# A query pipeline seven slots deep instead of nine, with a written timetable for its fill

## The chip, the core and the metric

The kernel runs on one core of one Trainium2 chip. The metric is the device time of one execution in microseconds (us). Three executions of the kernel before took 2966.6, 2970.59 and 2973.62 us; their median, 2970.59 us, is the time before.

The engines are called as the profile calls them: PE multiplies matrices (PEld loads its weights), DVE is the vector engine, ACT the scalar engine with the function tables, POOL the general one, SP the queue from which this kernel issues all its DMAs.

## The reference, cut to what matters

The input x has 8 sequences of 1024 tokens with 512 channels. It is normalized once, and two branches read the result: an encoder layer with Performer attention (16 heads of 32 channels, 128 random features) and an MLP of width 2048, and a channel mix that looks one token back.

```python
xn = _layernorm(x)                                     # no gain, no shift
# attention: phi(u) = exp(u @ omega.T - |u|^2/2 - max) / sqrt(128) + 1e-6
pq, pk = phi(q * 32**-0.25), phi(k * 32**-0.25)        # per head, per token
kv, z  = pk.T @ v, pk.sum(tokens)                      # over the whole sequence
h      = ((pq @ kv) / (pq @ z)) @ wo
a = layernorm(xn + h) * ln1_g + ln1_b
a = layernorm(a + gelu(a @ w1 + b1) @ w2 + b2) * ln2_g + ln2_b
# channel mix: p is xn one token back, zero at the start
r, k = sigmoid((mu_r*xn + (1-mu_r)*p) @ W_r), (mu_k*xn + (1-mu_k)*p) @ W_k
out = x + a + r * (square(relu(k)) @ W_v)
```

## The kernel before, in words

**Arithmetic.** Every large product is made from 16-bit halves: a value is held as a high and a low fp16 part, and a product is three matmuls (high x high, high x low, low x high). `mm3` (L139) is the unit of PE work: 12 matmuls of 128x512 over four chunks of 128 channels. Most engine work before and after it makes such pairs: ACT writes the high half, DVE or POOL subtracts to get the low one.

**Phase one, keys and channel mix.** Tokens come in tiles of 128 (`NU` = 64) and blocks of 512. Pools open and close around two phases that do not fit in memory together. In phase one each slot of 15.4 timetable microseconds (`us`, L191) normalizes a tile, makes V, a K projection (`proj_a`, tile name psu with weights whk), its features in two halves (`KB`, tile pj), and adds them into kv (`KC`, tile kac). Every eighth tile ends a sequence: `KD` and `KE` normalize kv and z of a head group and store them to DRAM (zd, epd). The channel mix, 192 `mm3` units named psk, psr and psf (`ffn_k`, `ffn_r`, `ffn_o`), is spread over the slots by the list `spots` (L904); its inputs come from `mix` (L550), and its results go to DRAM (ffd).

**Phase two, queries and MLP.** Query work is done per item i, which is a group of four heads over one block of 512 tokens; there are 64. An item goes through:
- `Lq`: load the block's normalized transposed tokens (tile xq, 1 MB, one buffer; every fourth item). The tile lies where phase one's pools lay.
- `proj_a`: one `mm3` (psu, weights whq); ACT and DVE make the pair u; SP writes it to DRAM (ud) and issues a DMA transpose of it.
- `proj_l`: three DMAs read ud back in another layout (skq). `norm`: POOL, ACT and DVE turn the transposed u into the squared norms (nsqq).
- `QB`, four times (t = 0 to 3): four small matmuls (pj<-oms,skq), DVE takes the maximum and the bias, ACT the exponentials, and a DMA transpose delivers the features (pq). pj has two buffers, eq three, pq four.
- `QD`, twice: 24 small matmuls with kv (acn<-zq,pq), then DVE divides. `QE`: ACT, POOL and a DMA transpose give oT.

For every block, four `O` units (pso, one per 128 tokens) apply wo; DVE adds the residual (x1), `bstat` and `rstat` make the layer norm, `pre` applies it and transposes the result into x1b. The MLP takes 64 slots, four per block n: in each, four `mlp1` units (psw0) with a GELU on ACT, and four `mlp2` units (acc, four PSUM banks). `fin_a` to `fin_b` finish and store a block.

**What sets the order.** Every step is an event with a time, `at(tau, ...)`; events are issued in order of tau. PE's instructions are chained in that order (`chained`, L129). DVE, ACT, POOL and SP are chained too (`Pinned`, L178), except between `unpin` at TK = 72.55 and `tail_banks` at TM = 81.6: there a list scheduler of the compiler orders them. Each engine then executes strictly in its order, waiting on semaphores. In the MLP slots `warp(j, t)` (L207) maps a place t in the nominal slot j (27.68 long, table `slot_pe`) to a tau, skipping PE work that the slot does not have.

Before, item i has its projection in MLP slot i-9, its features in slot i-8 and its products with kv in slot i-7. `O` of a block takes two slots, two units each.

Of the kernel before, what the change touches and what calls it, by code (L numbers as in the profile page):

```python
# [10 lines left out]
F32 = mybir.dt.float32  # L11
# [28 lines left out]
NU = NB * 8  # L40
# [11 lines left out]
TC = 78.8  # L52
TM = 81.6
QT = (0.68, 0.77, 0.86, 0.95)
QDT = (0.27, 0.49)
QDF = (0.45, 0.75)
QF = (0.10, 0.30, 0.52, 0.90)
# [3 lines left out]
def block_kernel(ctx, tc, x, wq, wk, wv, wo, om3, ln1_g, ln1_b, w1, b1, w2, b2,  # L61
# [84 lines left out]
    def tail_banks():  # L146
        for key in ("act", "dve", "gps", "spq"):
            pin[key] = None
# [46 lines left out]

    def slot_pe(j):
        q = j + 8
        o = 2 if j % 4 in (1, 2) and 0 < j < 59 else 0
        f = j < 4 * NBK
        return [(0.0, MM3 * f), (2.56, MM3 * f), (5.12, MM3 * (j > 0)), (7.68, 0.6 * (q - 1 < NU)),  # L200
                (8.28, MM3 * (q + 1 < NU)), (10.84, MM3 * f), (13.4, 0.6 * (q - 1 < NU)), (14.0, MM3 * o),
                (16.56, MM3 * f), (19.12, 0.22 * (q < NU)), (19.34, MM3 * (j > 0)), (21.9, 0.22 * (q < NU)),
                (22.12, MM3 * f), (24.68, 0.22 * (q < NU)), (24.9, MM3 * f), (27.46, 0.22 * (q < NU))]
# [18 lines left out]
    def Y(j, t):  # L222
        return 0 if j is None else (warp(j, t),)
# [180 lines left out]
    def proj_a(kind, b, u, j=None):  # L404
# [10 lines left out]
        yield us(2.65) if kind == "k" else Y(j, 10.9)  # L415
        u2 = st([128, 2, BLK], F16, "u2", U2_BUFS)
        act.activation(u2[:, 0, :], ps, AF.Copy, scale=sc)
        yield us(1.2) if kind == "k" else Y(j, 11.6)
        dve.scalar_tensor_tensor(u2[:, 1, :], ps, sc, u2[:, 0, :], ALU.mult, ALU.subtract)
        yield us(1.2) if kind == "k" else Y(j, 12.5)  # L420
# [6 lines left out]

    def norm(kind, b, u, j=None):
# [4 lines left out]
        yield us(4.0) if kind == "k" else Y(j, 27.68 + 7.2)  # L433
        act.activation(uu, uu, AF.Square, scale=1.0 / SU)
        yield us(5.0) if kind == "k" else Y(j, 27.68 + 9.6)
# [114 lines left out]
    def mix(bk, p, f):  # L550
# [5 lines left out]
        for w in range(2):  # L556
# [3 lines left out]
            yield us(2.0)  # L560
            df = st([128, BLK], F32, "df", 1)
            gps.tensor_tensor(df, xs[:, 1:BLK + 1], xs[:, 0:BLK], ALU.subtract)
            yield us(4.5)
            for nm, mu in (("k", muk), ("r", mur)):
                dve.scalar_tensor_tensor(
                    xm[nm][:, w], df, mu[:, c:c + 1], xs[:, 0:BLK], ALU.mult, ALU.add
                )
                yield us(2.0 * f)
            yield us(2.0 * f)
        cs = slice(p * 2, p * 2 + 2)  # L570
        for nm in "kr":
# [4 lines left out]
            yield us(3.0)  # L576
            dve.tensor_tensor(m[:, 1, cs, :], xm[nm], m[:, 0, cs, :], ALU.subtract)
            yield us(2.0 * f)
# [41 lines left out]
    def QB(b, u, t, j=None):  # L620
# [3 lines left out]
        sk, nsq = stk["q", b, u], nrm["q", b, u]  # L624
# [4 lines left out]
        yield Y(j, p + 0.3)  # L629
        mx = st([128, 4], F32, "mxq", 4)  # L630
        dve.tensor_reduce(mx, pj, AX.X, ALU.max)
        yield Y(j, p + 1.05)
        bi = st([128, 4], F32, "biq", 4)
        dve.scalar_tensor_tensor(bi, mx, -1.0 / (SU * SU), nsq[:, t * 4:t * 4 + 4], ALU.mult, ALU.add)
        yield Y(j, p + 1.3)
# [4 lines left out]
        yield Y(j, p + (3.9 if t == 0 else 3.1))  # L640
        eng = dve if QLO[t] == "v" else gps
        eng.tensor_tensor(eq[:, 1], e, eq[:, 0], ALU.subtract)
        yield Y(j, p + (5.3 if t == 0 else 4.2))
# [440 lines left out]
```

## Time and profile before

| | |
|---|---|
| median of three runs | 2970.59 us |
| profiled execution: time, span | 2970.69 us, 2968.9 us |
| PE busy | 2787.5 us (94%), 18784 matmuls |
| DVE, ACT, POOL busy | 2264.2, 1767.8, 1026.3 us |
| DMA | 839348 packets, 494.82 MB, mean 167 GB/s |
| end of the last matmul before the span's end | about 28 us |

The profile is one execution, taken by the hardware. Its page has busy time by engine, the span in 40 slices of 74 us each, the costliest groups of instructions and what the engine waited for before them. Because helpers issue all instructions, all matmuls stand under L137 and nearly all other instructions under L185; so they are told apart by tile names. "out<-in" names the tiles written and read, without buffer numbers. A bracket after a row is the idle time before it and what ended it. Landing is the time from a DMA's issue to its completion. Since PE's matmuls overlap, a busy PE is not a PE at full speed: the granted clock (1.0 is full) stands beside it.

### The profile page before, as it was taken

The page shows a single profiled execution, that of the slowest core. Times are in us where ns is not written, and L with a number is a line of the kernel's source. Part 1 is how long each engine was busy: PE and PEld are TensorE (multiplying, and loading weights), DVE is VectorE, ACT ScalarE, POOL GpSimd, SP SyncE. Part 2 cuts the span into 40 slices and gives each one's busy share as a digit, 9 for nine tenths or more (in the row PEclk, how much of TensorE's full clock was granted, in tenths as well). Part 3 has the DMA queues.
Part 4 walks back from the last instruction along what each step waited for, and adds up shares of the span by engine and source line. Part 5 has one row for each costly group of instructions (what it writes and reads, how often), then busy time and mean ns, then how long its engine had stood idle before and what let it go on. Part 6 is the DMA issues. An engine that isn't in the chain of part 4 may idle for free. (4 is left out here: it accounts for less than half of the span.)

```text
span 2968.9 us, 52134 instructions
## 1 busy us (share of the span) xinstructions
PE 2787.5 (94%) x18784; PEld 1390.3 (47%) x18784; DVE 2264.2 (76%) x4308; ACT 1767.8 (60%) x3892; POOL 1026.3 (35%) x945
## 2 busy tenths in 40 slices
PE   3999999999999785999999999999999999999996
PEld 1454445445555342444444444444444444444442
DVE  5888888888888656667777777778777777787554
ACT  4888888888888564455455455454554554554210
POOL 3454555555655233223223223223223232232111
PEclk7999999999999896999999999999999999999998
DMA  6566666666665288877777777777777687786432
GB/s 195 144 171 183 175 176 176 183 179 178 171 172 128 95 184 176 196 162 175 190 164 179 179 169 176 187 163 176 186 171 172 173 175 172 174 179 156 117 100 85
DMA packets 839348, 494.82 MB, mean 167 GB/s; under 512 B 632016, under 2 KB 718128, under 8 KB 837040
## 3 DMA queue, kind: packets, MB, share of 16 engines
q1 hardware_dynamic: 839088, 491.49, 66.6%
q8 instruction: 147, 2.41, 0.4%
q14 instruction: 113, 0.93, 0.1%
HBM read 226.95 MB, written 113.38 MB: 115 GB/s over the span
## 5 line engine op out<-in xcount | busy, mean ns | idle before, releaser
L137 PE MATMUL psw<-x1b,w1s 128*128 128x512 f16 x3072 | 696.5, 380 | 1.8 <-DVE u L185 1.8
L137 PE MATMUL acc<-w2h,gg 128*128 128x512 f16 x2048 | 648.1, 379 | 0.0
L137 PEld LDWEIGHTS <-w1s 128*128 128x128 f16 x3072 | 296.5, 98 | 346.3 <-issue 6.0
L137 PEld LDWEIGHTS <-gg 128*128 128x128 f16 x3072 | 292.7, 98 | 324.1
L185 ACT ACTIVATE g<-psw,b1t 128x512 f32<-128x512 f32 x256 | 173.0, 686 | 374.8 <-PE psw L137 363.5
L137 PE MATMUL acc<-w2l,gg 128*128 128x512 f16 x1024 | 387.9, 379 | 0.0
L185 ACT ACTIVATE e<-pj,biq 128x128 f32<-128x128 f32 x1024 | 291.0, 369 | 149.3 <-DVE biq L185 120.3
L185 ACT ACTIVATE e<-pj,bik 128x128 f32<-128x128 f32 x1024 | 287.9, 391 | 47.7 <-DVE bik L185 47.6
L185 POOL TENSOR_TENSOR eq<-e,eq 128x512 f16<-128x512 f32 x128 | 164.7, 1287 | 385.5 <-ACT eq L185 229.3
L185 DVE TENSOR_REDUCE mxq<-pj 128x4 f32<-128x512 f32 x256 | 175.5, 687 | 119.8 <-PE pj L137 118.7
L185 POOL TENSOR_TENSOR u<-ot,u 128x512 f16<-128x512 f32 x64 | 84.4, 1319 | 460.7 <-ACT u L185 422.1
L185 POOL TENSOR_TENSOR e<-u 128x512 f32<-128x512 f16 x128 | 163.9, 1281 | 107.2 <-DMA u<-u 92.0
L185 ACT ACTIVATE u<-psu 128x512 f16<-128x512 f32 x128 | 75.9, 593 | 207.8 <-PE psu L137 207.7
L185 DVE SCALAR_TENSOR_TENSOR gg<-g,gg 128x512 f16<-128x512 f32 x256 | 189.1, 739 | 8.8
L185 DVE TENSOR_SCALAR gg<-g 128x512 f16<-128x512 f32 x256 | 108.0, 422 | 104.6 <-ACT g L185 104.5
L137 PE MATMUL psv<-whv,xb 128*128 128x512 f16 x512 | 165.9, 386 | 18.7 <-ACT u L185 18.7
L137 PE MATMUL psu<-xb,whk 128*128 128x512 f16 x512 | 156.1, 387 | 28.7 <-DVE v L185 23.3
L185 POOL TENSOR_TENSOR xf<-xf,be 128x512 f32<-128x512 f32 x64 | 81.0, 1265 | 291.8 <-DMA xf<-in_x 172.5
L185 DVE SCALAR_TENSOR_TENSOR ekl<-e,ekh 128x1024 f16<-128x1024 f32 x128 | 177.3, 1385 | 4.5 <-ACT ekh L185 4.4
L185 ACT ACT_TABLE_LOAD x114 | 146.3, 1283 | 55.8 <-DVE biq L185 47.7
L137 PE MATMUL psr<-whfr,mx 128*128 128x512 f16 x512 | 165.9, 386 | 6.6 <-DVE v L185 3.9
L185 POOL TENSOR_TENSOR x<-x,bb 128x512 f32<-128x512 f32 x64 | 89.3, 1397 | 226.1 <-ACT u L185 165.6
(164 smaller groups left out, 5801.9 us busy)
## 6 DMA issues: line engine op xcount, KB each, us to landing
w1s<-w1d SPq DMA_DIRECT2D x256, 256.0 KB, 3.0
ud<-u SPq DMA_DIRECT2D x128, 256.0 KB, 2.2
skk<-ud SPq DMA_DIRECT2D x192, 128.0 KB, 2.8
skq<-ud SPq DMA_DIRECT2D x192, 128.0 KB, 3.2
xt<-in_x SPq DMA_DIRECT2D x64, 256.0 KB, 3.4
xnd<-xt SPq DMA_DIRECT2D x64, 256.0 KB, 2.4
xtd<-xb SPq DMA_DIRECT2D x16, 1024.0 KB, 5.2
ffd<-rsg SPq DMA_DIRECT2D x64, 256.0 KB, 2.2
```

The costliest lines, as they stand in the source:

```text
L137: return chained("pe", nc.tensor.matmul(*a, **k))
L185: return lambda *a, **k: chained(self.key, f(*a, **k))
```

## The change

All matmuls, vector instructions and DMAs of the computation stay; the change is in the order, in a few buffer counts, and in two more loads of the activation table.

- **Depth.** Item i's projection now stands in MLP slot i-7 (`LAG`), after the first psw0, and its features at the end of the same slot. Its products with kv stand in slot i-6, the first of them 2.56 later in the slot. Seven items, not nine, are projected before the first MLP unit.
- **Output projections.** The four `O` units of a block stand in one slot (j % 4 == 2), and `bstat`, `rstat`, `pre`, the final norms and their DMAs get new places.
- **Fill.** `unpin` is gone: all engines stay chained. Projections of items 0 to 6 stand at TQ + 0, 5.1, 10.2, 18.3, 29.1, 39.9, 50.7 (`PSQ`), an item's features start at 15.2 + 10 i, one QB per 2.5; `O` of block 0 stands at 74 to 82, the MLP starts at 102 instead of 9 slots of 15.4 (138.6).
- **Channel mix.** `spots` end with a list `wide` in the fill; `mix` is timed by shares of its interval. Between the last K projection and the first query projection there are 13 units instead of 15, from then to the first psw0 18 instead of 13, before both 161 instead of 164.
- **Smaller.** `KE` of the last sequence stands 2.6 later; xn has 3 buffers instead of 2, x1 10 instead of 11; new clock `rt`, which counts real PE time in a slot.

```diff
-TC = 78.8
-TM = 81.6
+TC = TQ + 73.0 / 15.4
+TM = TQ + 102.0 / 15.4
...
     def tail_banks():
-        for key in ("act", "dve", "gps", "spq"):
-            pin[key] = None
...
+    LAG = 7
+
     def slot_pe(j):
-        q = j + 8
-        o = 2 if j % 4 in (1, 2) and 0 < j < 59 else 0
+        q = j + LAG < NU
+        d = j + LAG - 1 < NU
+        o = 4 if j % 4 == 2 and j < 4 * NBK - 4 else 0
         f = j < 4 * NBK
-        return [(0.0, MM3 * f), (2.56, MM3 * f), (5.12, MM3 * (j > 0)), (7.68, 0.6 * (q - 1 < NU)),
-                (8.28, MM3 * (q + 1 < NU)), (10.84, MM3 * f), (13.4, 0.6 * (q - 1 < NU)), (14.0, MM3 * o),
-                (16.56, MM3 * f), (19.12, 0.22 * (q < NU)), (19.34, MM3 * (j > 0)), (21.9, 0.22 * (q < NU)),
-                (22.12, MM3 * f), (24.68, 0.22 * (q < NU)), (24.9, MM3 * f), (27.46, 0.22 * (q < NU))]
+        return [(0.0, MM3 * f), (2.56, MM3 * q), (5.12, MM3 * (j > 0)), (7.68, MM3 * f), (10.24, 0.6 * d),
+                (10.84, MM3 * f), (13.4, 0.6 * d), (14.0, MM3 * o), (16.56, MM3 * f), (19.12, 0.22 * q),
+                (19.34, MM3 * (j > 0)), (21.9, 0.22 * q), (22.12, MM3 * f), (24.68, 0.22 * q),
+                (24.9, MM3 * f), (27.46, 0.22 * q)]
...
+    def rt(j, t):
+        warp(j, 0.0)
+        ln = warps[j][1]
+        return TM + j + t / ln if t < ln else rt(j + 1, t - ln)
+
+    def Y(j, t, dt):
+        return us(dt) if j is None else (warp(j, t),)
+
+    def R(j, t, dt):
+        return us(dt) if j is None else (rt(j, t),)
...
-        yield us(2.65) if kind == "k" else Y(j, 10.9)
+        yield us(2.65) if kind == "k" else R(j, 5.2, 2.65)
-        yield us(1.2) if kind == "k" else Y(j, 11.6)
+        yield us(1.2) if kind == "k" else R(j, 6.0, 0.8)
-        yield us(1.2) if kind == "k" else Y(j, 12.5)
+        yield us(1.2) if kind == "k" else R(j, 6.8, 0.8)
...
+    def sqt(j):
+        if j is None or j % 4 > 1:
+            return R(j, 18.2 if j and j % 4 == 2 else 13.95, 0.8)
+        return Y(j, 19.0, 0)
...
-        yield us(4.0) if kind == "k" else Y(j, 27.68 + 7.2)
+        yield us(4.0) if kind == "k" else R(j, 11.8 if not j else (14.4, 14.4, 14.4, 13.0)[j % 4], 1.5)
-        yield us(5.0) if kind == "k" else Y(j, 27.68 + 9.6)
+        yield us(5.0) if kind == "k" else sqt(j)
...
-    def mix(bk, p, f):
+    def mix(bk, p, m0, m1):
+        def to(share):
+            return (m0 + share * (m1 - m0),)
...
-            for nm, mu in (("k", muk), ("r", mur)):
+            for nm, mu, f in (("k", muk, 0.21), ("r", mur, 0.28)):
+                yield to(f + 0.36 * w)
                 dve.scalar_tensor_tensor(
                     xm[nm][:, w], df, mu[:, c:c + 1], xs[:, 0:BLK], ALU.mult, ALU.add
                 )
-                yield us(2.0 * f)
-            yield us(2.0 * f)
+            yield to(0.36 + 0.36 * w)
...
-        sk, nsq = stk["q", b, u], nrm["q", b, u]
+        sk = stk["q", b, u]
...
+        nsq = nrm["q", b, u]
+        assert len(nsq.shape) == 2, (b, u, t, j)
...
-        yield Y(j, (8.4, 14.05)[p])
+        yield Y(j, 10.9, 0.7) if p == 0 else R(j, 14.05, 0.7)
...
-        yield Y(j, 16.5)
+        yield R(j, 15.95, 0.7)
...
-        xns[i] = sm_([128, D], F32, "xn", 2)
+        xns[i] = sm_([128, D], F32, "xn", 3)
...
-        x1 = sm_([128, D], F32, "x1", 11)
+        yield us(2.7) if tev is None else (tev,)
+        x1 = sm_([128, D], F32, "x1", 10)
...
-        yield Y(j, (2.7, 5.3, 13.5, 19.2)[k])
+        yield Y(j, 19.2, 0) if k == 3 else R(j, (2.7, 10.3, 13.5)[k], 0)
-        yield Y(j, (4.2, 6.0, 15.2, 23.2)[k])
+        yield Y(j, 23.2, 0) if k == 3 else R(j, (4.2, 12.0, 15.2)[k], 0)
...
-    def unpin():
-        for key in ("act", "dve", "gps", "spq"):
-            pin.pop(key, None)
...
-            at(i + 9 + us(7.65 if b < NB - 1 else 0.0), KE, b, u - 4)
+            at(i + 9 + us(7.65 if b < NB - 1 else 2.6), KE, b, u - 4)
...
-    spots = [c + us(o) for c in range(CM0, CM0 + 72) for o in (0.0, 5.12, 12.0)]
-    spots = [t for k, t in enumerate(spots) if k % 9 != 8]
+    PSQ = (0.0, 5.1, 10.2, 18.3, 29.1, 39.9, 50.7)
+    wide = [2.4 + 2.7 * k for k in range(24)]
+    wide = [TQ + us(t) for t in wide if min(abs(t - q) for q in PSQ) > 1.4]
+    spots = [c + us(o) for c in range(CM0, 73) for o in (0.0, 5.12, 12.0)]
+    spots = [t for t in spots if t < TQ - 0.05]
+    n = 12 * NBK - len(wide)
+    spots = [spots[k * len(spots) // n] for k in range(n)] + wide
...
-                at(m1, mix, bk, 1, ((tau - 0.3 - m1) * 15.4 - 19.0) / 14.0)
+                m1 = max((m0 + tau - 0.3) / 2, tau - 2.4)
+                at(m0, mix, bk, 0, m0, m1)
+                at(m1, mix, bk, 1, m1, tau - 0.3)
...
-    at(TK, unpin)
...
-        s, j = TQ + i, i - 9
+        j = i - LAG
         if j < 0:
-            e = 0.45 if i else 0
+            q = TQ + us(PSQ[i])
+            z = TQ + us(15.2 + 10.0 * i)
             if u % NG == 0:
-                at(s + 0.30 - e, Lq, b, u)
-            at(s + 0.31 - e, proj_a, "q", b, u)
-            at(s + 0.32 - e, proj_l, "q", b, u)
-            at(s + 0.96 - e, norm, "q", b, u)
+                at(q - us(0.1 if i == 0 else 8.0), Lq, b, u)
+            at(q, proj_a, "q", b, u)
+            at(q + us(6.6), proj_l, "q", b, u)
+            at(q + us(8.5), norm, "q", b, u)
         else:
             if u % NG == 0:
-                at(warp(j - 1, 11.0) if j else s - 0.4, Lq, b, u)
-            at(warp(j, 8.28), proj_a, "q", b, u, j)
-            at(warp(j, 15.6), proj_l, "q", b, u)
-            at(warp(j, 18.0), norm, "q", b, u, j)
+                at(rt(j - 1, 5.4) if j else TQ + us(70.0), Lq, b, u)
+            at(warp(j, 2.56), proj_a, "q", b, u, j)
+            at(rt(j, 9.6), proj_l, "q", b, u)
+            at(rt(j, 11.6 if j else 9.4), norm, "q", b, u, j)
         if u == 0:
-            at(s + 1.05, Lz, b)
+            at(z if i == 0 else rt(j, 8.0), Lz, b)
         for t in range(4):
+            if j < 0:
+                at(z + us(2.5 * t), QB, b, u, t)
+            else:
+                at(warp(j, (19.12, 21.9, 24.68, 27.46)[t]), QB, b, u, t, j)
+        for p in range(2):
             if j + 1 < 0:
-                at(s + 1 + QF[t], QB, b, u, t)
+                at(z + us((12.6, 18.6)[p]), QD, b, u, p)
             else:
-                at(warp(j + 1, (19.12, 21.9, 24.68, 27.46)[t]), QB, b, u, t, j + 1)
-        for p in range(2):
-            if j + 2 < 0:
-                at(s + 2 + QDF[p], QD, b, u, p)
-            else:
-                at(warp(j + 2, (7.68, 13.4)[p]), QD, b, u, p, j + 2)
-        if j + 2 < 0:
-            at(s + 2.80, QE, b, u)
+                at(warp(j + 1, (10.24, 13.4)[p]), QD, b, u, p, j + 1)
+        if j + 1 < 0:
+            at(z + us(20.0), QE, b, u)
         else:
-            at(warp(j + 2, 15.4), QE, b, u, j + 2)
+            at(rt(j + 1, 15.3), QE, b, u, j + 1)
...
-                tau = TQ + 6.5 + 0.3 * (t // 2) + 0.01 * (t % 2)
-                at(tau - 0.001, Ln2, t)
+                tau = TQ + us(74.0 + 2.6 * t)
+                at(TQ + us(73.2 + 0.2 * t if t < 3 else 77.0), Ln2, t)
                 at(tau, O, n, t)
-                at(TQ + 7.2 + 0.02 * t, bstat, "P", n, t)
+                at(tau + us(2.75), bstat, "P", n, t)
                 if t % 2:
-                    at(TQ + 7.21 + 0.02 * t, rstat, "P", n, t - 1)
-                at(TQ + 7.3 + 0.15 * t, pre, n, t)
+                    at(tau + us(3.6), rstat, "P", n, t - 1)
+                at(TQ + us((81.2, 81.9, 86.5, 87.2)[t]), pre, n, t)
             else:
-                j = 4 * n - 3 + t // 2
+                at(rt(j - 2, 6.0 + 0.3 * t if t < 3 else 17.0), Ln2, n * 4 + t)
+                at(warp(j - 2, 14.0 + 0.64 * t), O, n, t, warp(j - 2, 14.66 + 0.64 * t))
+                at(max(rt(j - 2, (17.35, 20.0, 23.1, 25.1)[t]), warp(j - 2, 14.67 + 0.64 * t)), bstat, "P", n, t)
-            at(warp(j - 3, 17.4), bstat, "P", n, 1)
-            at(warp(j - 2, 7.2), rstat, "P", n, 0)
-            at(warp(j - 1, 3.4), pre, n, 2, [warp(j - 1, t) for t in (7.0, 7.1, 12.7, 13.3)])
-            at(warp(j - 1, 10.4), pre, n, 3, [warp(j - 1, t) for t in (12.1, 12.2, 16.4, 17.6)])
+            at(rt(j - 2, 20.8), rstat, "P", n, 0)
+            at(rt(j - 2, 27.95), rstat, "P", n, 2)
...
+            for t, c in enumerate((
+                ((2, 33.5), (2, 34.2), (2, 35.2), (3, 6.8), (3, 7.6)),
+                ((3, 1.2), (3, 2.0), (3, 4.9), (3, 7.5), (3, 8.3)),
+                ((3, 8.2), (3, 8.9), (3, 9.7), (3, 13.2), (3, 14.0)),
+                ((3, 9.6), (3, 10.3), (3, 11.1), (3, 16.45), (3, 17.3)),
+            )):
+                w = [rt(j - 4 + r, v) for r, v in c]
+                at(w[0], pre, n, t, w[1:])
...
-            tau = warp(s, (0.0, 2.56, 10.84, 16.56)[k])
+            tau = warp(s, (0.0, 7.68, 10.84, 16.56)[k])
-                at(tau - 1.0 if fc > 3 else TM - 5.0 + fc, get_w1, n, fc)
+                at(tau - 1.0 if fc > 3 else TM - us(20.0 - fc), get_w1, n, fc)
...
-                at(warp(j + 5, (1.3, 7.2, 10.5, 12.7)[t]), bstat, "F", n, t)
-            at(warp(j + 5, 20.4), rstat, "F", n, 0)
+                at(rt(j + 5, (1.3, 6.8, 7.65, 8.5)[t]), bstat, "F", n, t)
+            at(rt(j + 5, 9.35), rstat, "F", n, 0)
...
```

## The prediction

> **What bounds the kernel now.** I read the page's slices first: where does PE not run, or run cold?
>
> ```profile
> PE   3999999999999785999999999999999999999996
> ...
> PEclk7999999999999896999999999999999999999998
> ```
>
> PE is full almost everywhere; the holes are the start, slices 14 to 16 (the hand-over from keys to queries) and the end. The stretches that follow are cut at the last K items, at the first query projection and at the first MLP unit.
>
> ```profile
> core 0: us, PE busy (x) PEld busy (x) DVE busy (x) ACT busy (x) POOL busy (x), PEclk, DMA share, GB/s
> ...
> 972.00:1036.00 64.00, 47.44 (x341) 23.53 (x340) 44.22 (x61) 34.74 (x75) 19.14 (x18) 0.87 0.27 82
> 1036.00:1181.00 145.00, 98.82 (x778) 51.63 (x777) 88.94 (x198) 77.10 (x203) 46.97 (x39) 0.81 0.84 187
> ...
> 1205.00:2900.00 1695.00, 1685.08 (x10816) 825.85 (x10815) 1277.32 (x2703) 824.24 (x1688) 434.86 (x339) 1.00 0.71 168
> ```
>
> Busy time flatters PE, so I count work by spacing at full clock: an mm3 unit in the timeline takes 2.59 us from start to start (psf at 1033.42, next unit at 1036.01), the small pj, acn and kac matmuls 0.055, 0.025 and about 0.028 us each. Then the **drain** (972 to 1036) holds 14 units, 32 pj and 141 kac matmuls = 42 us of work in 64: 22 lost. The **fill** (1036 to 1181) holds 26 units, 130 pj, 336 acn = 83 us in 145: 62 lost. In the **main stretch** PE issues without holes; its waits sum to about 10 us, and with small gaps I count 14. What is lost in the drain and fill, and to whom:
>
> ```profile
> PE kac L137 <- DVE kvz L185: 14.8, 4, 9.0
> ...
> PE pj L137 <- ACT e L185: 23.0, 8, 7.2
> PE acn L137 <- DMA pq<-eq: 22.2, 5, 7.1
> ```
>
> The first row is the drain's, the others the fill's. Only the start, these two stretches and the last 28 us offer time; start and end are not touched. The rest is PE work that the change keeps, unit for unit.
>
> **The change part by part.** The sum is made on the profiled execution, 2970.7 us (span 2968.9), equal to the median to 0.1.
>
> *Drain.* Two psr units now stand between the last feature groups, where before PE had nothing:
>
> ```profile
> 982.48 0.61 PE L137 MATMUL pj<-oms,skk 96*128 96x128 f16 x8
> 984.67 0.61 PE L137 MATMUL pj<-oms,skk 96*128 96x128 f16 x8 [1.58 <-ACT e L185]
> 994.24 0.60 PE L137 MATMUL kac<-kvz,ones 128*128 128x132 f16 x2 [8.96 <-DVE kvz L185]
> 994.63 1.06 PE L137 MATMUL psk<-mx,whfk 128*128 128x512 f16 x2
> ```
>
> From zmean (978.98) to the ready kvz (994.24) DVE needs 15.3 us; PE now has 9.6 us of work there instead of 4.4, so of the 9 us some 5 stay, and of the later waits (2.0 and 4.3) perhaps 2. But the three units that stood after the last kac are gone: the projection follows it at once, and its input can only be loaded when the last store of phase one has landed:
>
> ```profile
> 1027.06 0.32 SPq L185 DMA_DIRECT2D epd<-eps  x1
> ...
> 1030.13 0.32 SPq L185 DMA_DIRECT2D xq<-xtd  x1
> ```
>
> xq landed 4.8 us after its issue (1034.94); the last kac ended at 1026.72. So PE will stand 8.2 us, now uncovered. Everything behind it on PE waits with it (units of the channel mix too), and on SP ud and skq queue behind xq. After a hole the clock is low: the psk unit at 994.63 took 5.0 us instead of 2.59, 2.4 us more. Lost after: 5 + 2 + 8.2 + 2.4 = 17.6, against 22. I take -5. Bounds: no wait but the hole (8.2 lost) -14; all old waits and the hole, +6. The trace is nearest to the middle, since the DVE chain is the same work.
>
> The Trainium skill (TensorE: Matmul & The Clock Gate, Part 1) says that an idle window of about 3.4 us halves the clock and that a busy one of that length restores it, so it speaks against the naked hole; by it the price of the hole's cold restart is at most 1.7 us instead of the row's 2.4, and the sum 0.7 lower.
>
> *Fill.* PE's work from first projection to first psw0 becomes 7 + 18 + 4 = 29 units, 112 pj, 288 acn = 88.5 us. The timetable gives it 102. Can the others keep that pace? Durations of the main stretch's rows: ACT 112 exponentials at 0.28, 28 copies at 0.62, the rest, about 76 us; DVE 84; POOL 44; SP 45 transposes at 1.25 and 21 skq at 0.45 plus the rest, about 80. All fit, none with much to spare. DMA does not fit:
>
> ```profile
> skq<-ud SPq DMA_DIRECT2D x27, 128.0 KB, 2.5
> ud<-u SPq DMA_DIRECT2D x9, 256.0 KB, 2.6
> ...
> pq<-eq SPq DMA_TRANSPOSE x30, 3.3
> ...
> u<-u SPq DMA_TRANSPOSE x9, 3.0
> oT<-u SPq DMA_TRANSPOSE x6, 3.3
> x1b<-u SPq DMA_TRANSPOSE x4, 2.8
> ```
>
> Before's fill kept the DMA engines busy for 0.84 x 145 = 122 us with 49 transposes; the new one has 45 (28 + 7 + 6 + 4), so 122 x 45/49 = 112 us, more than 102. At a share of 0.95 it takes 118. Lost: 118 - 88.5 = 29.5 instead of 62: **-32.5**. Ends: the timetable is kept (packets are stretched by crowding, so 112 may be too much), -48; the features come at before's pace of some 3.9 us a QB (32 between 1046 and 1172), 15 + 28 x 3.9 + 28 = 152 us, +2. I take the DMA share, because it counts the same transfers. Five channel-mix units move here from places with no slack: nothing by themselves, being counted in the work.
>
> The Trainium skill (DMA: Bandwidth & Descriptors, Latency and other measured facts) gives 261 GB/s for DMA transposes, which makes one of 256 KB an estimated 1.0 us and all 45 only 45 us; by it DMA would not bind, the timetable would hold and the sum would be lower by 16.
>
> *Main stretch.* Three things change. (1) Features in the slot of their projection. After psu, PE has acc, psw0, acn, psw0, acn, psw0 = 11.6 us before the first pj waits for skq (22 in the slot with pso). The chain: at the first projection before, psu started at 1036.01 and pj ran at 1046.37 without a wait, so at most 7.6 us after psu's 2.76. In the main stretch add up to 1.5 us for ACT's and DVE's queues (a GELU pair is ahead), and behind DVE's u wait SP's ud, the transpose and skq; in slot j % 4 == 3 two x1b transposes (2.5 us) stand between. That is 8 to 11.5 us: covered. Not so every fourth slot, where xq goes out just ahead of ud:
>
> ```profile
> 1245.21 0.32 SPq L185 DMA_DIRECT2D xq<-xtd  x1
> 1247.12 0.32 SPq L185 DMA_DIRECT2D ud<-u  x1
> ```
>
> Here ud landed 5.9 us after its issue; over the 13 such pairs it was 4.1 to 6.8, elsewhere in the middle 2.15. That brings the chain to about 11.5 to 13 us, and all that PE has in order behind pj (acc, the other pj, psw0) waits with it: I price 0.5 us in 14 slots, 7 us, plus 3 for jitter elsewhere. (2) QD's first half comes 2.56 later: it gains most of the 6.8 us that acn waited for pq in the main stretch, say 4. (3) Four pso in a row: DVE must clear one per 2.59 us (0.69 us each, 2.1 us of layer norm between); with two psum banks the slack is 1.8 us, and I put it at nothing. DVE's work in that slot is about 33 of 35 us; if a wait comes, the next pso bears it. The first MLP slots get 1 us less cover, no price; two more table loads (1.28 each) are hidden by ACT's 49% idle time. x1's smaller pool, xn's third buffer, edits of final norms: off PE's path, nothing. Sum 7 + 3 - 4: **+6**. Bounds: all waits go, -10; a microsecond in each of the 43 short slots, +43.
>
> *Phase one.* 164 against 161 units, `mix` moved: DVE and ACT are at 85 to 87% there and PE loses about 43 us in 824. Nothing, -6 to +6.
>
> Sum: 2970.7 - 5 - 32.5 + 6 = **2939**.
>
> **Rivals.**
> - *The timetable holds* (2924): fill at 102. For it: no engine but PE (88.5) is over 84 us. Against: 0.84 of DMA busy already at a slower pace.
> - *The fill is not compressed* (2960 to 2972): the order is fixed but the pace is DMA's and the pq ring's, as in before, where pq waits were 22 us and pj waited 23 on ACT. For it: share 0.84 over the whole fill; against: that time was spent partly behind a bad order, with 39 us between the last pso and the first psw0.
> - *Slower: the same-slot features starve PE* (about 2985 to 3005). Place: the first pj of a slot, waiting for skq. Each microsecond over the 11.6 of cover costs 43 us over the short slots; against a gain of 37.5 it decides from 0.9 us a slot, a chain of 12.5. For it: ud and skq landings are 2.2 and 3.2 at best, SP is a single queue, and DMA is busy at 0.71; against: the measured 7.6.
>
> **How the numbers follow.** Forecast case (2925 to 2957) 0.56; timetable held or better 0.11; fill hardly shorter 0.16 (of it 0.10 faster, 0.05 same, 0.01 slower); starvation 0.17. Faster by over 0.2% (6 us, about what a measurement of this kernel can tell from no change) 0.77, within 0.05, slower 0.18. The range 2912 to 2978 leaves out about 0.06 below (drain, fill and main all at their good ends give 2899) and 0.14 of the starvation case above. The forecast's own range is 2925 to 2957.
>
> **What would show it.** Right: the fill from first whq projection to first psw0 takes 110 to 125 us with DMA share over 0.9; a PE hole of about 8 us ahead of the first whq projection, ended by xq; in the main stretch pj waits for skq in every fourth slot, under 1 us each, and acn waits shrink. Wrong: pj waits of a microsecond in all short slots, or psw0 and pso waiting for DVE's x1, or a fill over 140.

## The result: slower, 3101.0 us

The changed kernel takes 3101.03 us (median of 4 runs, 3099.33 to 3103.01), the kernel before beside it 2971.12: a ratio of 1.0439, 95% interval 1.0421 to 1.0457. The forecast was 2939. The profiled execution took 3100.28 us, its span is 3098.5. In the changed file all matmuls stand under L133 and the other instructions under L179.

First the slices of the page after, PE busy and granted clock:

```profile
PE   4999999999998858999999999999999999999997
...
PEclk8999999999999878999999999999999999999998
```

They look hardly different: the same two dark slices, and nines after them. Work per stage tells more. I count it as in the prediction (full-clock work by the spacing of matmuls, 2737.6 us in both kernels) and call lost what a stage takes beyond it. K phase is from 148 us to 64 us before the first whq projection, the drain is those 64, the fill ends at the first psw0, the main stretch 105 us before the last matmul.

| lost, us | before | after | change | forecast |
|---|---|---|---|---|
| start, to 148 us | 59.0 | 57.6 | -1.4 | 0 |
| K phase | 43.2 | 33.6 | -9.6 | 0 |
| drain | 21.9 | 18.4 | -3.5 | -5 |
| fill | 62.0 | 71.2 | +9.2 | -32.5 |
| main stretch | 16.4 | 159.8 | +143.4 | +6 |
| last 105 us of matmuls | 0.3 | 0.6 | +0.3 | 0 |
| behind the last matmul | 28.4 | 19.6 | -8.8 | 0 |

The changes add up to 129.6 us, the difference of the two spans. So the question is the main stretch. Drain, fill, first 50 us and main stretch of the changed kernel, by stretches of the trace:

```profile
core 0: us, PE busy (x) PEld busy (x) DVE busy (x) ACT busy (x) POOL busy (x), PEclk, DMA share, GB/s
945.00:1009.00 64.00, 48.62 (x363) 24.70 (x362) 48.27 (x68) 40.18 (x89) 25.51 (x25) 0.93 0.24 73
1009.00:1168.50 159.50, 103.82 (x748) 52.29 (x747) 91.84 (x187) 76.74 (x189) 42.86 (x35) 0.81 0.69 154
1168.50:1219.00 50.50, 42.81 (x278) 20.24 (x279) 21.41 (x44) 18.91 (x37) 7.09 (x6) 0.91 0.76 190
1219.00:2969.00 1750.00, 1651.59 (x10461) 800.57 (x10460) 1307.57 (x2643) 807.91 (x1682) 431.89 (x335) 0.97 0.66 159
```

The main stretch ran without holes at a clock of 1.00 before; now PE is 98 us idle in it and the clock is 0.97. The waits of PE there (1200 to 2950), in us, times and longest:

```profile
PE pj L133 <- ACT e L179: 47.9, 14, 4.0
PE pso L133 <- DVE x L179: 44.5, 13, 4.6
PE pj L133 <- DMA skq<-ud: 6.7, 5, 4.5
```

Two waits, each once per block of four slots, each some 3.5 us. The wait that I feared (pj for skq) is small; that for pq, 6.8 before, is gone. To see in which slots they fall, I took the start of the first psw0 unit of each MLP slot from the timeline and averaged slots 4 to 55 by place in the block (13 each). DVE busy is the time in which at least one of its operations runs; neighbouring ones overlap a little, so the sum of their durations is larger (26.1 us in slot 3 after, the figure in the expectation of e2_late_bb2):

| slot j % 4, us | before | after | DVE busy before | DVE busy after |
|---|---|---|---|---|
| 0 | 26.0 | 25.6 | 20.8 | 16.1 |
| 1 | 30.6 (2 pso) | 25.5 | 21.5 | 20.9 |
| 2 | 30.6 (2 pso) | 40.9 (4 pso) | 25.1 | 31.0 |
| 3 | 25.4 | 31.1 | 20.3 | 24.7 |
| block | 112.6 | 123.1 | 87.7 | 92.7 |

At full clock slot 2 of the changed kernel needs 25.4 + 4 x 2.59 = 35.7 and slot 3 needs 25.4: each loses some 5 us per block.

**Slot 2.** One instance on DVE's timeline, and the pso on PE that waits:

```profile
1602.71 0.69 DVE L179 SCALAR_TENSOR_TENSOR gg<-g,gg 128x512 f16<-128x512 f32 x1
1609.82 1.62 DVE L179 SCALAR_TENSOR_TENSOR xf<-xf 128x512 f32<-128x512 f32 x1 [6.42 <-POOL xf L179]
...
1613.46 0.68 DVE L179 SCALAR_TENSOR_TENSOR x<-xn,pso 128x512 f32<-128x512 f32 x1
```
```profile
1614.19 0.58 PE L133 MATMUL pso<-who,oT 128*128 128x512 f16 x1 [4.64 <-DVE x L179]
1614.57 0.63 PE L133 MATMUL pso<-wlo,oT 128*128 128x512 f16 x1
...
1617.56 0.63 PE L133 MATMUL pso<-who,oT 128*128 128x512 f16 x2
```

DVE stands 6.42 us with a final norm's xf at the head of its queue (`fin_b`, fourth tile). Behind it, in order, are nm, gg and the evacuation x<-xn,pso (DVE reads a finished pso out of its PSUM bank, so that PE can use the bank again), which needed nothing but DVE. This is the longest of 15 such waits. Before that POOL stood too, for the loads that xf adds up:

```profile
1601.34 0.58 SPq L179 DMA_DIRECT2D xf<-ffd  x1
1602.02 0.39 SPq L179 DMA_DIRECT2D xf<-in_x  x1
```
```profile
1608.53 1.26 POOL L179 TENSOR_TENSOR xf<-xf,be 128x512 f32<-128x512 f32 x1 [11.59 <-DMA skq<-ud]
```

The row names a skq load as what ended POOL's wait, but the second xf load itself landed 6.3 us after its issue, at 1608.37, just before the add. The timetable gives 3.9 us from the load to the add; the add began 6.5 us after the second load's issue. The loads were late too: SP issued the first 11.3 us into the slot instead of 7.6, behind a transpose of pq, three loads of xn, the store of ud and the transpose of u.

After the hole matmuls start 0.43 us apart instead of 0.21 until 1617.56, for 3.4 us, at half speed, which loses 1.6 us. Over the main stretch (1200 to 2950) 10 of the 13 holes ahead of a pso leave such slow matmuls behind them, for 2.9 to 5.4 us, 17.8 us lost in all; three holes (3.0, 2.2 and 2.2 us long) leave none. The mean hole of 3.4 us and a mean of 1.4 us lost behind it are about the 5 us a slot. The Trainium skill (TensorE: Matmul & The Clock Gate, Part 1) has the same behaviour: an idle window of about 3.4 us halves the clock, and a busy one of about that length restores it. The case agrees in kind; in size the runs decide, since here holes of 2.3 us were enough and some restarts took 5.4 us.

**Slot 3** has the three other `pre` steps, each three DVE operations. DVE's groups with the layer norm, before (first fence) and after (second), mean ns behind the busy time:

```profile
L185 DVE SCALAR_TENSOR_TENSOR x<-x,mvP,g 128x512 f32<-128x512 f32 x56 | 41.7, 745 | 0.0
```
```profile
L179 DVE SCALAR_TENSOR_TENSOR x<-x,mvP,g 128x512 f32<-128x512 f32 x57 | 68.1, 1195 | 0.0
```

The same operation takes 1195 ns instead of 745. In the timeline of one such slot (DVE, POOL):

```profile
1641.03 1.75 DVE L179 SCALAR_TENSOR_TENSOR x<-x,mvP,g 128x512 f32<-128x512 f32 x1
1642.82 1.65 DVE L179 SCALAR_TENSOR_TENSOR x<-x,rsP,be 128x512 f32<-128x512 f32 x1
1644.38 1.64 DVE L179 SCALAR_TENSOR_TENSOR x<-x,mvP,g 128x512 f32<-128x512 f32 x1
1646.06 0.75 DVE L179 SCALAR_TENSOR_TENSOR x<-x,rsP,be 128x512 f32<-128x512 f32 x1
...
1654.54 0.68 DVE L179 TENSOR_REDUCE mxq<-pj 128x4 f32<-128x512 f32 x1
```
```profile
1640.65 3.26 POOL L179 TENSOR_TENSOR x<-x,bb 128x512 f32<-128x512 f32 x2 [6.48 <-DVE u L179]
1643.87 1.60 POOL L179 TENSOR_TENSOR e<-u 128x512 f32<-128x512 f16 x1
```

While POOL works, the DVE operations take 1.64 to 1.75 us, and 0.75 as soon as it has stopped. So DVE is busy 24.7 us in a slot that PE would leave after 25.4, with hardly any room to wait: mxq comes 5 us after its pj (which ended at 1649.4), the exponentials after it, and PE's third pj waits (1658.53, 3.67 us for ACT e).

### The profile page after: what moved, and what is told of

The parts are those of the page before. It is cut to its first block, busy times and chain, and to the rows that moved or that the text cites. A ratio compares the mean times of both kernels' runs of the same rounds, so it can differ in the third digit from the quotient of the medians.

```text
span 3098.5 us, 52140 instructions
## 1 busy us (share of the span) xinstructions
PE 2830.6 (91%) x18784; PEld 1399.6 (45%) x18784; DVE 2320.6 (75%) x4308; ACT 1760.4 (57%) x3894; POOL 1022.9 (33%) x945
## 5 line engine op out<-in xcount | busy, mean ns | idle before, releaser
L133 PE MATMUL psw<-x1b,w1s 128*128 128x512 f16 x3072 | 705.2, 380 | 26.8 <-DMA x1b<-u 25.2
L133 PE MATMUL acc<-w2h,gg 128*128 128x512 f16 x2048 | 665.5, 388 | 0.0
L179 ACT ACTIVATE g<-psw,b1t 128x512 f32<-128x512 f32 x256 | 174.5, 684 | 578.9 <-PE psw L133 569.1
L133 PEld LDWEIGHTS <-gg 128*128 128x128 f16 x3072 | 298.7, 100 | 339.6 <-issue 28.3
L133 PEld LDWEIGHTS <-w1s 128*128 128x128 f16 x3072 | 290.6, 98 | 354.1 <-issue 30.5
L133 PE MATMUL acc<-w2l,gg 128*128 128x512 f16 x1024 | 396.8, 387 | 0.0
L179 ACT ACTIVATE e<-pj,biq 128x128 f32<-128x128 f32 x1024 | 291.4, 367 | 144.0 <-DVE biq L179 139.1
L179 POOL TENSOR_TENSOR eq<-e,eq 128x512 f16<-128x512 f32 x128 | 155.5, 1214 | 601.4 <-ACT eq L179 597.8
L179 ACT ACTIVATE e<-pj,bik 128x128 f32<-128x128 f32 x1024 | 290.1, 407 | 33.2 <-DVE bik L179 33.1
L179 POOL TENSOR_TENSOR e<-u 128x512 f32<-128x512 f16 x128 | 164.9, 1288 | 288.0 <-DMA u<-u 286.4
L179 DVE TENSOR_REDUCE mxq<-pj 128x4 f32<-128x512 f32 x256 | 175.0, 684 | 83.6 <-PE pj L133 83.3
L133 PE MATMUL pso<-who,oT 128*128 128x512 f16 x512 | 171.9, 409 | 45.6 <-DVE x L179 45.6
L179 DVE TENSOR_SCALAR gg<-g 128x512 f16<-128x512 f32 x256 | 113.9, 445 | 131.5 <-ACT g L179 131.5
L179 POOL TENSOR_TENSOR xf<-xf,be 128x512 f32<-128x512 f32 x64 | 81.8, 1278 | 374.6 <-DMA xf<-in_x 260.6
L179 DVE SCALAR_TENSOR_TENSOR gg<-g,gg 128x512 f16<-128x512 f32 x256 | 193.3, 755 | 8.8
L133 PE MATMUL psv<-whv,xb 128*128 128x512 f16 x512 | 166.3, 386 | 21.2 <-ACT u L179 19.2
L133 PE MATMUL psu<-xb,whk 128*128 128x512 f16 x512 | 157.5, 390 | 28.8 <-DVE v L179 19.6
L179 DVE SCALAR_TENSOR_TENSOR ekl<-e,ekh 128x1024 f16<-128x1024 f32 x128 | 173.7, 1357 | 5.3 <-ACT ekh L179 5.1
L133 PE MATMUL pj<-oms,skq 96*128 96x128 f16 x1024 | 102.2, 223 | 79.2 <-ACT e L179 68.2
L179 DVE TENSOR_REDUCE mxk<-pj 128x8 f32<-128x1024 f32 x128 | 155.4, 1214 | 21.1 <-PE pj L133 20.8
L179 ACT CAST eq<-e 128x512 f16<-128x512 f32 x256 | 158.2, 618 | 19.5 <-DMA pq<-eq 8.7
```

What stands on the lines that cost most here:

```text
L133: return chained("pe", nc.tensor.matmul(*a, **k))
L179: return lambda *a, **k: chained(self.key, f(*a, **k))
```

## The experiments

Theory: in the main stretch the loss is made in DVE's in-order queue, in slot 2 at its head (xf), in slot 3 by operations that POOL lengthens; in the fill it is made at the head of SP's queue. Rivals: four output projections in one slot are too many in themselves; features in the slot of their projection starve PE; the feature chain has its own pace. Ratios are to the kernel before in the same session (2970 to 2972 us).

**One move on DVE and POOL.** In `fin_b`'s table, fourth tile:

```diff
-(rt(m,7.6), rt(m, 11.5), rt(m, 13.1), rt(m, 26.0), rt(m, 26.7), rt(m, 27.6)),
+(rt(m,7.6), rt(m, 21.0), rt(m, 25.3), rt(m, 26.0), rt(m, 26.7), rt(m, 27.6)),
```

> The changed kernel; of the fourth final norm only, GpSimd's add into xf and VectorE's xf operation move from 11.5 and 13.1 us of the slot with four output projections to 21.0 and 25.3, behind the pso evacuations. Same work. In the changed kernel this slot lasts 40.9 us, where its matmuls at full clock are about 35.5, and pso waits for x 13 times, 44.5 us. Theory 'queue head': VectorE stands idle behind that xf (68.7 us in the main stretch) and the pso evacuations stand behind it; then the pso wait falls under 10 us, the slot to about 36, and with the cold clock after each hole 14 x 4 to 5 us go: 3030 to 3045. Rival 'VectorE too slow for four pso in a row' (evacuation, batch norm statistics, the rest between): the wait stays over 30 us and the time within 3085 to 3110. The pj wait (47.9 us, the slot after) stays in both.

Measured 3043.57 us, ratio 1.0242 (1.0227 to 1.0257): 57 us less. Slot 2 lasts 35.8 us, the pso wait is gone, and of DVE's 68.7 us at xf this is left (1230 to 2950):

```profile
DVE xf L179 <- POOL xf L179: 0.6, 1, 0.6
```

DVE is still busy 30.7 us in that slot, so it was not short of time. The theory holds. In the trace 44.5 us of holes and 17.8 of restarts go; slot 3 takes some of it back, where the pj wait for ACT e grows from 47.9 to 51.8.

**The bb additions a slot later.** In `pre`:

```diff
+        yield us(2.0) if ts is None else (rt(4 * n, (4.5, 8.5, 17.5, 21.5)[t]),)
         gps.tensor_tensor(x1, x1, cst["bb2"], ALU.add)
```

> The changed kernel; only the four additions of bb on GpSimd that follow the x1b transposes are moved one slot later, into the slot where GpSimd is busy 4.8 us of 25.6. Same work. In the slot after the four output projections VectorE is busy 26.1 us where the matmuls need 25.3, and x<-x,mvP,g takes 1.20 us on average there against 0.745 in the kernel before; the long ones (1.65) lie beside GpSimd's additions. Theory 'collision': the mean falls to 0.75 to 0.85, the slot from 31.1 to about 27, the pj wait under 20 us: 3040 to 3065. Rival 'too much VectorE work in one slot': durations may fall but the pj wait stays over 35 us: 3085 to 3100. The pso wait (44.5 us) stays in both.

Measured 3059.16 us, ratio 1.0287 (1.0267 to 1.0308): 42 us less. The operation and the waits of PE (1230 to 2950):

```profile
L179 DVE SCALAR_TENSOR_TENSOR x<-x,mvP,g 128x512 f32<-128x512 f32 x60 | 45.6, 760 | 0.0
```
```profile
PE pso L133 <- DVE x L179: 46.4, 13, 4.7
PE pj L133 <- ACT e L179: 9.0, 15, 0.9
```

Slot 3 is down to 26.3 us, DVE busy in it 21.5. The collision of the two engines in this slot was the cause; the other hole stays as it was.

> Both moves of the two runs above. If the two holes are separate and are what the main stretch lost, the gains add: 2975 to 3010, and the main stretch loses under 50 us instead of 146. If one hole only uncovers another limit (SyncE's queue, skq in the slot of its projection), less than 70 us are gained: over 3030.

Both together: 2994.31 us, ratio 1.0079 (1.0064 to 1.0094), 107 us less; the sum of the two gains is 99, the same within the intervals. The main stretch loses 47.9 us. What is left of waits in it:

```profile
PE pj L133 <- DMA skq<-ud: 10.9, 13, 1.6
PE pj L133 <- ACT e L179: 9.0, 15, 1.1
PE pj L133 <- DVE ot L179: 4.3, 4, 1.3
```

**Output projections two and two again.** One part of the change undone:

```diff
-    LAG = 7
+    LAG = 8
...
-        o = 4 if j % 4 == 2 and j < 4 * NBK - 4 else 0
+        o = 2 if j % 4 in (1, 2) and 0 < j < 59 else 0
```

with the kernel before's times for `Ln2`, `O`, `bstat`, `rstat` and `pre`, its buffer counts for xn and x1, and eight units in the fill (timetable 10 us longer).

> The changed kernel with one part undone: two output projections in each of two slots as before, with the kernel before's times for their loads, statistics and x1b steps; for that the pipeline needs eight units in the fill instead of seven (10 us more in its timetable). Features stay in the slot of their projection. Theory 'four output projections in one slot cause both holes': pso and pj waits both fall under 20 us, main stretch near the kernel before's: 2975 to 3005. Rival 'features in the slot of their projection starve PE': the pj wait stays over 35 us, 3060 or more. Rival 'the xf order alone': only the pj wait falls, pso keeps its 40 us: 3040 to 3060.

Measured 3052.97 us, ratio 1.0268 (1.0253 to 1.0283). My theory of that row fails: the main stretch still loses 85 us. The time is the one forecast for the rival 'the xf order alone', and the pj wait for ACT e does fall, to 18.2 us; but the wait for DVE's evacuation is halved and stands at another matmul (1301 to 2950):

```profile
PE psw L133 <- DVE x L179: 23.5, 13, 3.7
```

It is the psw0 behind the second pso, waiting for the evacuation, which stands behind the same xf (DVE waits 22.6 us for it, 13 times). So it is not the number of output projections alone. This run also has another timetable for the layer norm and an eighth item in the fill; so the same kernel with the two moves:

> The kernel of e5_two_o (3053: output projections two and two, eight units in the fill) with the two moves of e3_both: the fourth final norm's xf operations behind the pso evacuations, the four additions of bb one slot later. In e5_two_o the main stretch after its first 50 us lost about 80 us; VectorE waits 22.6 us at that same xf there, and psw0 behind it 23.5 us for x. Theory 'the heads of the queues cost, not four output projections in one slot': its main stretch falls to what e3_both loses (38 us) or a little over, 3005 to 3020 in all. Rival 'two and two is better or worse in itself': under 25 us lost in the main stretch (below 3000) or over 60 (above 3030).

Measured 3018.81 us, ratio 1.0159 (1.0141 to 1.0177). Its main stretch loses 48.0 us, that of e3_both 47.9: two and two or four in a row cost the same once the queues' heads are free. It is 24 us behind e3_both elsewhere: K phase 60.1 lost instead of 32.9, fill 78.4 instead of 72.5, drain 15.4 instead of 20.4. Why the K phase depends on the eighth unit was not looked into.

**The fill.** It took 160 us in the changed kernel, 102 by its timetable. SP in its early part:

```profile
1044.04 2.52 SPq L179 DMA_TRANSPOSE pq<-eq  x1
1054.02 1.27 SPq L179 DMA_DIRECT2D skq<-ud  x3
1055.39 1.23 SPq L179 DMA_TRANSPOSE pq<-eq  x1
```

From 1046.6 to 1054.0 SP stands at a skq load whose buffer (one of two) a pj still reads. The pq transpose behind it had its eq ready at 1050.1 on POOL; acn and ACT's eq then wait 4.3 and 4.4 us for it. Between 1045 and 1140 SP waits 17.8 us for pj in this way:

```profile
SPq L179 <- PE pj L133: 17.8, 3, 8.4
```

Two runs on top of e3_both: the loads later, or the whole order of DVE, ACT, POOL and SP left to the scheduler as before (the expectations call it the planner).

```diff
-            at(q + us(6.6), proj_l, "q", b, u)
+            at(max(q + us(6.6), z - us(11.8)), proj_l, "q", b, u)
```

> The kernel of e3_both (2994); in the fill only, the three skq loads of units 2 to 6 are placed 8.2 us after the start of the features of the unit two before, when the skq buffer (two of them) comes free, instead of 6.6 us after their own projection. Nothing else moves. In the changed kernel SyncE waits 17.8 us for pj at these loads (the first time 7.4 us), with pq transposes behind them; acn waits 9.9 us for pq and ScalarE's eq 8.7. Theory 'SyncE's queue head sets the fill's pace': those waits fall under 5 us each, the fill from 161 to 138 to 150, the time 2972 to 2985. Rival 'the transposes themselves come too slowly' or 'the other engines' order': the fill stays over 155, 2988 to 3000.

Measured 2985.34 us, ratio 1.0052 (1.0039 to 1.0065), at the edge of the forecast; fill 161 to 147 us. SP's wait for pj falls to 2.4 us, and PE no longer waits for pq in the fill. It still waits for ACT e (19.2 us, hardly changed), ACT now 33.1 us for DVE's bias (22.4 in the changed kernel), SP 16.3 for DVE eq (1045 to 1140): the next links of the chain. Of the 14 us in the fill 9 show in the time; in this profile the main stretch loses 8 us more than in e3_both.

```diff
+    at(TK, unpin)
```

(with `unpin` and the reset of the chains in `tail_banks` as in the kernel before)

> The kernel of e3_both (2994) with one part of the change undone: between the end of phase one and the first MLP slot the order of VectorE, ScalarE, GpSimd and SyncE is again left to the planner, as in the kernel before; TensorE's order is the timetable's. In e3_both the fill (first whq psu to first psw0) takes 161 us for 28 feature groups, 72 us more than its matmuls. Theory 'an order written out by hand blocks the queues' (SyncE stands for pj with pq transposes behind it, VectorE for ScalarE): the planner's order takes 125 to 145, the time 2960 to 2980. Rival 'the pace is that of the feature chain itself, about 4 us a group in either order': 155 to 165, 2985 to 3005.

Measured 2975.46 us, ratio 1.0014 (1.0003 to 1.0025); fill 134 us (first line e3_both, second this run):

```profile
1010.70:1171.80 161.10, 104.99 (x748) 52.34 (x748) 91.33 (x187) 76.94 (x189) 42.30 (x35) 0.81 0.69 152
1009.80:1143.90 134.10, 98.73 (x748) 50.62 (x749) 88.17 (x185) 73.67 (x188) 42.51 (x35) 0.86 0.84 184
```

The same operations, 27 us less: the written order was the brake, not the chain's own pace. Only 19 of the 27 show in the time; in this profile the main stretch loses 14 us more than in e3_both, and pj waits 18.0 us for skq in it instead of 10.9. Why was not looked into.

**Projection ahead of the first psw0**, on top of e3_both:

```diff
-        return [(0.0, MM3 * f), (2.56, MM3 * q), (5.12, MM3 * (j > 0)), ...
+        return [(0.0, MM3 * q), (2.56, MM3 * f), (5.12, MM3 * (j > 0)), ...
...
-                at(rt(j - 1, 5.4) if j else TQ + us(70.0), Lq, b, u)
+                at(rt(j - 1, 9.0) if j else TQ + us(70.0), Lq, b, u)
```

and the steps of both units shifted by 2.55 us.

> The kernel of e3_both (2994); in each slot the query projection stands ahead of the first psw0 unit instead of behind it, with ScalarE's, VectorE's and SyncE's steps of the projection 2.55 us earlier and those of the first psw0 2.55 later, and xq is loaded after ud and skq instead of just ahead of ud. So the chain to the first pj has about 2.6 us more cover. In e3_both pj waits 28 us in the main stretch after its start, 11 of them for skq, 9 for ScalarE, 8 named after VectorE, and the stretch loses 44 us against 14 in the kernel before. Theory 'same-slot features cost about a microsecond a slot': the skq waits fall under 3 us and the time to 2960 to 2980 (with 2.6 us from a projection in the hole before the first psw0). Rival 'what is left is jitter of the queues': 2985 to 3000.

Measured 2971.96 us, ratio 1.0007 (0.9995 to 1.0019): 22 us less. One row of PE's waits is left in the main stretch (1220 to 2900), none for skq:

```profile
PE pj L133 <- ACT e L179: 24.5, 24, 1.9
```

In the two profiles, which lie 14 us apart, the main stretch went from 47.9 to 36.0 us lost, 5 of these 12 in its first 50 us, and the fill from 72.5 to 66.7 (PE has a projection in the hole before the first psw0), while the K phase, which the edit does not touch, lost 6.5 more. So the theory's "about a microsecond a slot" is not shown: 12 us over 57 slots with a projection are 0.2 each, and PE's waits between 1220 and 2900 fall only from 28.9 to 24.5, since the wait for ACT e grows as the one for skq goes. The edit also moves the load of xq behind ud and skq; which of the two moves took the skq waits away is not told apart.

**Together**: first the edits of f2_skq_late and f3_psu_first, then those of f1_unpin and f3_psu_first, then all three, each on top of e3_both.

> The edits of f2_skq_late and f3_psu_first together. If fill and main stretch are separate, the gains add: 2945 to 2970, so faster than the kernel before. If either rival holds, 2970 to 2990.

Measured 2958.35 us, ratio 0.9961 (0.9948 to 0.9973): the gains add, 36 us against 9 + 22, within the intervals.

> The kernel of e3_both (2994) with the edits of f1_unpin (-19, fill 161 to 134 us) and f3_psu_first (-22): fill ordered by the planner, projection first in the slot. If the two are separate, the gains add: 2950 to 2960, 10 to 20 us ahead of the kernel before. If the planner's order at the end of the fill and the projection in the hole before the first psw0 get in each other's way: 2960 to 2975.

Measured 2954.20 us, ratio 0.9941 (0.9924 to 0.9957).

> As g1_unpin_psu, and the planner is given the skq loads of the fill at the later times of f2_skq_late. If SyncE's head still costs something under the planner's order (it waited 4.2 us for pj in f1_unpin, acn 8.6 us for pq), 2945 to 2955; if the planner had found an order as good by itself, the same as g1_unpin_psu within 4 us.

Measured 2949.27 us, ratio 0.9928 (0.9913 to 0.9942). It is the fastest, 21 us ahead of the kernel before, but its interval overlaps that of g1_unpin_psu, so what the later loads add under the scheduler is not told apart. In its profile the fill takes 133 us and the main stretch loses 34.8:

```profile
1012.40:1145.60 133.20, 101.07 (x760) 51.58 (x760) 88.63 (x186) 74.16 (x189) 42.34 (x35) 0.86 0.86 186
```

Last, on top of f5_skq_psu:

> The kernel of f5_skq_psu (2958, fill 145 us, order by the timetable), with two more operations taken from the head of a queue in the fill: VectorE's wlo operations of the output projection's weights 1.2 us behind ScalarE's who instead of right behind it (VectorE waits 7.1 us for who, with mxq and biq behind), and the four constant vectors loaded after the first xn instead of ahead of them (VectorE waits 4.5 us for xn). Theory 'each in-order queue stands at its head': fill 145 to 136 to 142, time 2949 to 2955. Rival 'the slack goes to the next engine in the chain': 2955 to 2960.

```diff
+                    if nm == "o":
+                        yield us(1.2)
                     dve.scalar_tensor_tensor(wl[:, c, :], t, SW, wh[:, c, :], ALU.mult, ALU.subtract)
...
-    at(TC, mlp_consts)
+    at(TQ + us(74.2), mlp_consts)
```

Measured 2952.10 us, ratio 0.9935 (0.9920 to 0.9950), fill 138 us: two more heads freed, 7.5 us less in the fill, in a written order that now comes close to the scheduler's. The intervals of the two ratios, this one and that of f5_skq_psu, just touch.

## Why the prediction was wrong, point by point

Of its own signs of being wrong two came: pso waits for DVE's x, and the fill takes over 140 us.

- **Drain**, -5 forecast, -3.5 measured. The hole stands where it was put, with its size (8.2 forecast, 7.9 measured), and the waits for kvz and kvr together are 6.9 against 5 + 2 (945 to 1009). Behind the hole 11 matmuls start 0.43 us apart, 2.3 us lost: the 2.4 taken from a row was right, the bound of 1.7 that I had worked out from the skill's page (TensorE: Matmul & The Clock Gate, Part 1) too low:

```profile
PE psu L133 <- DMA xq<-xtd: 7.9, 1, 7.9
PE kac L133 <- DVE kvr L179: 3.5, 2, 3.3
PE kac L133 <- DVE kvz L179: 3.4, 3, 1.3
```

- **Fill**, -32.5 forecast, +9.2 measured. The amount of DMA work was right (112 us forecast, 0.69 x 159.5 = 110 measured). The step that failed is "At a share of 0.95 it takes 118": nothing kept the engines at that share, and the share was 0.69. SP, which issues every transfer, stood at its head; freeing that gives 14 us (f2_skq_late), leaving the whole order to the scheduler 27 (f1_unpin). I had judged each engine by its sum of work and not by what stands at the head of its queue. The second rival (fill not compressed) is what happened, for a reason that it did not name. Its upper end was also read too low: the first 31 QBs of the kernel before start between 1046.5 and 1172.0, 4.2 us apart and not 3.9, which makes 161 us instead of 152; that this comes near the 159.5 shows nothing of the cause. Even under the scheduler's order the share is 0.84 to 0.86 and the fill 133 to 134 us, so 118 was not near; what keeps these last 16 us stays open. The last 25 us of the changed kernel's fill are the layer norm behind the last pso, a wait of PE that stands in the upper end of the forecast alone (28); in f1_unpin it is 18.6. On one point the estimate that the prediction worked out from the Trainium skill's 261 GB/s (DMA: Bandwidth & Descriptors, Latency and other measured facts) was nearer: DMA did not bind, since the same transfers took 27 us less in f1_unpin; but the timetable of 102 us did not hold either. PE's waits in the fill of the changed kernel (1005 to 1175):

```profile
PE psw L133 <- DMA x1b<-u: 25.2, 1, 25.2
PE pj L133 <- ACT e L179: 19.2, 8, 4.9
PE acn L133 <- DMA pq<-eq: 9.9, 6, 4.3
```

- **Main stretch**, +6 forecast, +143.4 measured: 111.9 that the two moves of e3_both take away, and 31.5 that stay. "(3) Four pso in a row ... I put it at nothing" held for the projections themselves (e1_late_xf, h1_two_o_both), but the next line, "edits of final norms: off PE's path, nothing", is the step that failed: one xf operation moved in front of the evacuations costs about 57 us (e1_late_xf). The sentence "if a wait comes, the next pso bears it" named the place and gave it no price. The second part was not in the sum at all: the layer norm steps, three of four of which now fall into the slot behind the projections, and POOL's additions beside them, 42 us (e2_late_bb2). I did not count DVE's work slot by slot for them. (1) The price of the waits for skq was right: 7 in the slots where xq goes out ahead of ud and 3 elsewhere; in e3_both, free of both holes, they are 10.9 us, 6.5 of them in these slots. What the sum lacks of the 31.5 is elsewhere: about 7 us in the first 50 us of the stretch ("The first MLP slots get 1 us less cover, no price"), and 17.6 us in which pj waits for ACT or DVE (1220 to 2900). How much of this last comes from features in the slot of their projection is open. (2) The waits of acn for pq went, as forecast.
- **Phase one**, 0 within 6 forecast, -11 measured; the cause was not tested.
- **Two readings** of the prediction are off, without weight for the sum: 49% is ACT's busy share in the main stretch (824 of 1695 us), not its idle one, and 3.2 us is the median landing of skq, the shortest being 2.4.
- **The end**, called untouched, gained 8.8 us between the last matmul and the last instruction. In both kernels the last DVE operations wait for POOL xf in turn; that the changed kernel finishes the final norms of the block before the last one earlier would explain it, but this is only argued.
- **The slower rival** (pj starved by skq, 2985 to 3005) had the right sign and the wrong place: 6.7 us of such waits. A rule that would have spoken against the second part of the loss (POOL's additions beside DVE's layer norm, 42 us) stands in the Trainium skill (SBUF — State Buffer, Who interferes with whom): a DVE instruction with two SBUF inputs and a GpSimd instruction that reads SBUF exclude each other, the later one waits for the whole of the first. The case agrees: x<-x,mvP,g takes 0.745 us alone, 1.64 to 1.75 beside POOL in the slot shown; x<-xn,pso, with one input in PSUM, keeps 0.67 to 0.69 in all 64 cases, 15 of them beside POOL. I had weighed two rules on clock and DMA instead.

## What to carry to other kernels

In a kernel whose engines run in a written order, ask of every moved instruction what it will wait for and who stands behind it in its queue; the engine's share of busy time says nothing on that, and an operation with nothing to do with the bound engine can cost a hole in each round. Where a moved group of operations fills a slot to within a few per cent, count each engine's work slot by slot, with the durations it will have beside the other engine on its port. Leave slack between a load and the first instruction that reads it by the longest landing seen, not by the median.

## What the runs showed of the hardware

A hole on PE costs more than its length: behind 10 of 13 waits for pso (44.5 us in all, 2.2 to 4.6 each) the matmuls ran at half speed for 2.9 to 5.4 us, 17.8 us more; taking these waits away gave 57 us, 4.4 for each 3.4. DVE and POOL lengthen one another: 1195 against 745 ns on DVE, 3.26 us for two of POOL's additions that take 1.26 us each alone. And a busy DMA does not show what limits it: in the fill the share was 0.69 under the written order and 0.84 under the scheduler's (f1_unpin) for the same transfers, 110 and 113 us of engine time.
